# Count of candidates and casts of list and degree moved from VectorE to ScalarE, degree not clamped, replacement into a second buffer

## Chip, cores, metric

One core of a Trainium2 chip. The metric is the device time of one execution in microseconds; a profile's span is about 2 us shorter than the time of the same execution. Runs carry a state: "fast" or "slow" (over 1.5% above the fastest run of the same kernel). A ratio is the mean time of one kernel's fast runs over the mean of the other's fast runs of the same rounds, so it is not quite the ratio of the medians quoted beside it.

## The reference

One pre-norm graph-attention layer over N = 3327 nodes of width 1024. `adj` is 0/1 with few ones in a row.

```python
def reference(x, adj, Wf, bf, Wg, bg, W, bW):
    h = jnp.maximum(_layernorm(x, axis=-1), 0.0)
    f = h @ Wf + bf
    g = h @ Wg + bg
    e = jax.nn.relu(f @ g.T)
    scores = jnp.where(adj > 0, e, -9e15)
    return x + jax.nn.softmax(scores, axis=1) @ (h @ W + bW)
```

The kernel makes a list of the neighbours of each row (at most 40), sorts the rows by degree, and in part two gathers only those neighbours' rows.

## The kernel before

The change touches part one alone: 26 row tiles t0 to t25 (128 rows each, the last one 127). For each tile, `degrees` loads 128 rows of `adj`; ScalarE converts them to f32 and sums them to the degree (the "degree pass", L435); POOL multiplies by the column numbers in place (the "product", L436). `normed` is the layer norm, with small hand-overs between ScalarE and VectorE. In `edges`, VectorE searches 16 segments of the product for their 8 largest (the "searches", L446), counts the positive candidates, draws the list of 40 out of the 128 candidates by five maxima and four replacements (the "list"), and makes the list and the degree integer for a store.

```python
kpool = pool1("key", 4)     # the tiles r
cpool = pool1("cand", 2)    # cand, pos, ... : two buffers each

def normed(t):
    ...                     # even t: sums on ScalarE, odd t: statistics on VectorE
        nc.vector.bn_aggr(mv[:n], st[:n])
        nc.scalar.activation(nmr[:n], mv[:n, 0:1], AF.Copy, scale=-1.0)              # L409
    ...
    nc.vector.reciprocal(rstd[:n], rstd[:n])                                         # L419
    nc.scalar.activation(nmr[:n], nmr[:n], AF.Copy, scale=rstd[:n])                  # L420
    nc.scalar.activation(xt[:n], xt[:n], AF.Relu, bias=nmr[:n], scale=rstd[:n])      # L421
    ...

def degrees(t):
    r = kpool.tile([P, N], FP, name="r")
    ...                                                                              # load adj into r
    nc.scalar.activation(r[:n, b:e], a[:n, b:e], AF.Relu, accum_out=to)              # L435
    nc.gpsimd.tensor_mul(r[:n, b:e], r[:n, b:e], iotaj[:n, b:e])                     # L436
    ...

def edges(t, r):
    cand = cpool.tile([P, SEG * 8], FP, name="cand")
    for s in range(SEG):                                                             # SEG = 16
        nc.vector.max(cand[:n, s * 8 : s * 8 + 8], r[:n, s * SW : min(N, (s + 1) * SW)])
    pos = cpool.tile([P, SEG * 8], BF, name="pos")
    ...                                                                              # count, list, casts: see the diff

for t in range(NT):
    r = degrees(t)
    normed(t)
    edges(t, r)
    ...                                                                              # ranks, weights
```

This text is the order of tracing. The compiler's tile scheduler sorts the instructions of each engine into the queue that the engine then works off in order, so the order on the chip is not the order of these lines.

Of the kernel before, what the change touches and what calls it, by code (L numbers as in the profile page):

```python
# [8 lines left out]
FP = mybir.dt.float32  # L9
I32 = mybir.dt.int32  # L10
AF = mybir.ActivationFunctionType
ALU = mybir.AluOpType
AX = mybir.AxisListType
# [7 lines left out]
SEG = 16  # L21
KM = 40
NBIN = 64
# [266 lines left out]
def edge_path(ctx: ExitStack, tc: tile.TileContext, x, adj, Wf, bf, Wg, bg, W, bW, out, flag):  # L290
# [10 lines left out]
    nc = tc.nc  # L301
    N, D = x.shape
    O = W.shape[1]
    P = 128
# [4 lines left out]
    NT = (N + P - 1) // P  # L309
# [4 lines left out]
    def rows(t):  # L314
        return min(P, N - t * P)
# [7 lines left out]
    const = ctx.enter_context(tc.tile_pool(name="const", bufs=1))  # L323
# [10 lines left out]
    nc.gpsimd.iota(iotak, pattern=[[1, KM]], base=0, channel_multiplier=0, allow_small_or_imprecise_dtypes=True)  # L334
    ones3 = const.tile([3, P], BF, name="ones3")
    nc.gpsimd.memset(ones3, 1.0)
    bads = const.tile([P, NT + 2], FP, name="bads")
    nc.gpsimd.memset(bads, 0.0)


# [1 line left out]
    perm = const.tile([P, NT], I32, name="perm")  # L342
# [8 lines left out]
    with ExitStack() as part1:  # L351
        pool1 = lambda name, bufs, **kw: part1.enter_context(tc.tile_pool(name=name, bufs=bufs, **kw))
        c1 = pool1("c1", 1)
# [5 lines left out]
        cpool = pool1("cand", 2)  # L359
# [12 lines left out]
        iotad, lst = held[:, :NBIN], held[:, NBIN:]  # L372
# [9 lines left out]
        pay = c1.tile([P, NT, PW], I32, name="pay")  # L382
        deg = c1.tile([P, NT], FP, name="deg")
        half = c1.tile([P, 1], FP, name="half")
        cnt = c1.tile([P, NT], FP, name="cnt")
        rp = c1.tile([P, NT], FP, name="rp")
        oh = c1.tile([P, NT, NBIN], BF, name="oh")
# [53 lines left out]
        def edges(t, r):  # L441

            n = rows(t)
            cand = cpool.tile([P, SEG * 8], FP, name="cand")
            for s in range(SEG):
                nc.vector.max(cand[:n, s * 8 : s * 8 + 8], r[:n, s * SW : min(N, (s + 1) * SW)])  # L446
            pos = cpool.tile([P, SEG * 8], BF, name="pos")
            nc.vector.tensor_scalar(
                pos[:n], cand[:n], 0.0, None, op0=ALU.is_gt, op1=ALU.add, accum_out=cnt[:n, t : t + 1]
            )  # L450
            for i in range(0, KM, 8):
                nc.vector.max(lst[:n, i : i + 8], cand[:n])
                if i + 8 < KM:
                    nc.vector.match_replace(cand[:n], lst[:n, i : i + 8], cand[:n], 0.0)
            nc.vector.tensor_scalar(lst[:n], lst[:n], float(N), 1.0, op0=ALU.min, op1=ALU.max)
            nc.vector.tensor_scalar(pay[:n, t, :KM], lst[:n], -1.0, None, op0=ALU.add)
            dg = cpool.tile([P, 1], FP, name="dg")
            nc.vector.tensor_scalar(dg[:n], deg[:n, t : t + 1], float(NBIN - 1), None, op0=ALU.min)
            nc.vector.tensor_copy(pay[:n, t, KM : KM + 1], dg[:n])
            nc.vector.tensor_scalar(oh[:n, t, :], iotad[:n], dg[:n], None, op0=ALU.is_equal)  # L460

        def counted(t):

# [91 lines left out]
# [4 lines that stand above are left out]
            if t >= LAG:  # L559
                counted(t - LAG)  # L560
            if t % 4 == 3 and t > 4:
                store_lists(t - 7, t - 3)
            if t < KD:
                load_Wg(t)
            elif t < 2 * KD:
                make_A(t - KD)
            if t == 2 * KD:
                make_rows()
# [32 lines left out]
        ps = p_u.tile([P, P], FP, name="ps_u")  # L601
# [4 lines left out]
            )  # L606
        tens = c1.tile([P, NT], FP, name="tens")
        nc.vector.tensor_copy(tens, ps[:, NT : 2 * NT])
        nc.vector.scalar_tensor_tensor(perm, ps[:, :NT], float(P), tens, op0=ALU.mult, op1=ALU.add)
        over = c1.tile([P, 1], FP, name="over")  # L610
        nc.vector.tensor_scalar(over, part, float(rows(NT - 1)), float(N), op0=ALU.is_ge, op1=ALU.mult)
        nc.vector.tensor_tensor(final, perm[:, NT - 1 : NT], over, op=ALU.add)
        ne = c1.tile([P, NT], FP, name="ne")
        nc.vector.tensor_tensor(ne, deg, cnt, op=ALU.not_equal)
        nc.vector.tensor_reduce(bads[:, NT : NT + 1], ne, AX.X, ALU.max)
        nc.vector.tensor_scalar(ne, deg, 1.0, None, op0=ALU.is_lt)
        nc.vector.tensor_reduce(bads[:, NT + 1 : NT + 2], ne, AX.X, ALU.max)


    W_sb = ctx.enter_context(tc.tile_pool(name="W", bufs=1)).tile([P, KD, O], FP, name="W_sb")  # L620
# [204 lines left out]
def kernel(tc: tile.TileContext, x, adj, Wf, bf, Wg, bg, W, bW, out):  # L825



    nc = tc.nc
    with tc.tile_pool(name="flag", bufs=1) as fpool:  # L830
        flag = fpool.tile([1, 1], I32, name="flag")
        bad = edge_path(tc, x, adj, Wf, bf, Wg, bg, W, bW, out, flag)
        with tc.If(bad > 0):
            dense_path(tc, x, adj, Wf, bf, Wg, bg, W, bW, out)
# [27 lines left out]
```

## Time and profile before

| | before |
|---|---|
| time, median of 4 fast runs | 1421.8 us (1416.2 to 1423.8) |
| span of the profile, clock of TensorE granted | 1418.9 us, 0.923 |
| part one: start of the first gather on POOL | 285.9 us |
| POOL idle before its 28 products (L436) | 67.1 us |

### The profile page before, as it was taken

The page shows a single profiled execution, that of the slowest core. Times are in us where ns is not written, and L with a number is a line of the kernel's source. Part 1 is how long each engine was busy: PE and PEld are TensorE (multiplying, and loading weights), DVE is VectorE, ACT ScalarE, POOL GpSimd, SP SyncE. Part 2 cuts the span into 40 slices and gives each one's busy share as a digit, 9 for nine tenths or more (in the row PEclk, how much of TensorE's full clock was granted, in tenths as well). Part 3 has the DMA queues.
Part 4 walks back from the last instruction along what each step waited for, and adds up shares of the span by engine and source line. Part 5 has one row for each costly group of instructions (what it writes and reads, how often), then busy time and mean ns, then how long its engine had stood idle before and what let it go on. Part 6 is the DMA issues. An engine that isn't in the chain of part 4 may idle for free.

```text
span 1418.9 us, 14086 instructions
## 1 busy us (share of the span) xinstructions
PE 1176.7 (83%) x4355; PEld 686.1 (48%) x4355; DVE 1252.2 (88%) x2602; ACT 444.5 (31%) x686; POOL 872.4 (61%) x628
## 2 busy tenths in 40 slices
PE   4569998177298989999978987999999998999676
PEld 3544454044165556665545554555555554555332
DVE  4888889929979999998889889999999998999991
ACT  6666776311053134433302322212222111111100
POOL 8677777265666776665556546567666765656500
PEclk9999999578599999999989998999999998999788
DMA  9897796197677988886687567788887876788700
GB/s 370 334 361 301 290 350 220 48 368 269 223 286 265 328 313 310 285 277 245 233 308 280 201 236 274 271 297 297 279 288 245 266 251 224 245 281 264 256 31 32
DMA packets 97709, 372.51 MB, mean 263 GB/s; under 512 B 14268, under 2 KB 14684, under 8 KB 94297
## 3 DMA queue, kind: packets, MB, share of 16 engines
q0 software_dynamic: 79552, 286.85, 58.0%
q1 hardware_dynamic: 10860, 70.49, 13.1%
q10 hardware_dynamic: 7212, 14.18, 2.8%
q8 instruction: 36, 0.59, 0.2%
q14 instruction: 49, 0.40, 0.1%
HBM read 343.67 MB, written 27.80 MB: 262 GB/s over the span
## 4 chain that ended last, share of the span: by engine, by line
PE 28%; DVE 25%; issue 22%; POOL 15%; DMA 6%; ACT 2%; POOLq 0%; ACTq 0%; SPq 0%; DVEq 0%
PE ps_o L760 14%; DVE y L746 13%; POOL r L436 10%; PE ps_q L666 8%; DVE junk L683 6%; PE yT_ps L724 4%; POOL G L638 4%; DMA G<-hd,pi 4%; DVE cand L446 2%; PE ps_A L519 1%; DVE xp L768 1%; DVE sc L683 1%; DMA pi<-pd,perm 1%; ACT r L435 1%; PE ps_o L761 1%
## 5 line engine op out<-in xcount | busy, mean ns | idle before, releaser
L638 POOL DMA_INDIRECT G<-hd,pi x468 | 555.6, 1187 | 319.3 <-ACT y L744 105.9
L683 DVE CUSTOM_DVE_ANT_0 junk<-G,q 128x1024 bf16<-128x1024 f32 x468 | 600.6, 1283 | 41.4 <-DMA G<-hd,pi 21.6
L666 PE MATMUL ps_q<-A_sb,hT 128*128 128x342 f32 x1248 | 395.9, 467 | 58.1 <-ACT q L668 44.5
L746 DVE SCALAR_TENSOR_TENSOR y<-G,sc,y 128x1024 f32<-128x1024 f32 x320 | 411.2, 1285 | 4.4 <-ACT y L744 2.8
L760 PE MATMUL ps_o<-W_sb,yT 128*128 128x512 f32 x832 | 388.2, 621 | 10.2 <-ACT yT L755 9.9
L666 PEld LDWEIGHTS ps_q<-A_sb,hT 128*128 128x128 f32 x1248 | 233.5, 194 | 178.6 <-ACT q L668 46.3
L760 PEld LDWEIGHTS ps_o<-W_sb,yT 128*128 128x128 f32 x832 | 161.2, 198 | 209.4 <-issue 190.7
L436 POOL TENSOR_TENSOR r<-r,iotaj 128x3327 f32<-128x3327 f32 (+4 forms) x28 | 188.6, 6742 | 67.1 <-ACT r L435 53.1
L446 DVE MAX8 cand<-r 128x8 f32<-128x208 f32 (+2 forms) x416 | 134.2, 359 | 35.6 <-POOL r L436 35.6
L668 ACT COPY q<-ps_q 128x342 f32<-128x342 f32 x78 | 32.8, 449 | 326.2 <-DVE sc L683 234.6
L740 ACT ACTIVATE G<-G,sc 128x1024 f32<-128x1024 f32 x122 | 129.0, 1136 | 0.0
L519 PE MATMUL ps_A<-WgT,WfT 128*128 128x512 f32 x256 | 120.7, 633 | 1.1 <-ACT WfT L490 1.0
L724 PE MATMUL yT_ps<-ident,G 128*128 128x128 f32 x976 | 117.5, 277 | 2.4 <-ACT G L740 2.4
L724 PEld LDWEIGHTS yT_ps<-ident,G 128*128 128x128 f32 x976 | 107.5, 141 | 15.1 <-ACT G L740 7.3
L650 ACT COPY hT<-ps_t 128x512 f32<-128x512 f32 x52 | 30.2, 593 | 193.8 <-PE ps_q L666 162.9
L755 ACT COPY yT<-yT_ps 128x512 f32<-128x512 f32 x52 | 27.8, 586 | 194.3 <-PE yT_ps L724 194.3
L519 PEld LDWEIGHTS ps_A<-WgT,WfT 128*128 128x128 f32 x256 | 51.3, 203 | 65.0 <-issue 62.7
L724 PE MATMUL yT_ps<-ident,y 128*128 128x128 f32 x208 | 34.6, 321 | 52.8 <-DVE y L746 31.9
L435 ACT ACTIVATE r<-r 128x3327 f32<-128x3327 int32 (+4 forms) x28 | 77.5, 2766 | 0.1
L769 POOL DMA_INDIRECT out_dram<-xp,perm x25 | 31.8, 1271 | 59.4 <-DVE xp L768 50.9
L768 DVE TENSOR_TENSOR xp<-ps_o,xp 128x512 f32<-128x512 f32 x52 | 35.6, 685 | 36.0 <-PE ps_o L761 35.7
L724 PEld LDWEIGHTS yT_ps<-ident,y 128*128 128x128 f32 x208 | 28.7, 166 | 57.4 <-DVE y L746 34.6
(139 smaller groups left out, 781.0 us busy)
## 6 DMA issues: line engine op xcount, KB each, us to landing
r<-in_adj_dram SPq DMA_DIRECT2D x25, 1663.5 KB, 9.5
xt<-in_x_dram SPq DMA_DIRECT2D x25, 512.0 KB, 9.7
hd<-xt ACTq DMA_DIRECT2D x25, 512.0 KB, 6.1
G<-hd,pi POOLq DMA_INDIRECT x468, 6.1
wr<-in_L_gnn_Wg_dram SPq DMA_DIRECT2D x8, 512.0 KB, 13.8
wr<-in_L_gnn_Wf_dram SPq DMA_DIRECT2D x8, 512.0 KB, 8.9
W_sb<-in_L_gnn_W_dram SPq DMA_DIRECT2D x1, 4096.0 KB, 16.9
r<-in_adj_dram SPq DMA_DIRECT2D x1, 1455.6 KB, 8.7
```

Source lines behind the costliest of these rows:

```text
L435: nc.scalar.activation(r[:n, b:e], a[:n, b:e], AF.Relu, accum_out=to)
L436: nc.gpsimd.tensor_mul(r[:n, b:e], r[:n, b:e], iotaj[:n, b:e])
L446: nc.vector.max(cand[:n, s * 8 : s * 8 + 8], r[:n, s * SW : min(N, (s + 1) * SW)])
L519: nc.tensor.matmul(ps, WfT[:, k, :], WgT[:, k, o * CB : (o + 1) * CB], start=(k == 0), stop=(k == KD - 1))
L638: nc.gpsimd.indirect_dma_start(out=to, out_offset=None, in_=table, in_offset=bass.IndirectOffsetOnAxis(ap=idx, axis=0),)
L666: nc.tensor.matmul(ps[:, :QB], hT[:, k, :], A_sb[:, k, o : o + QB], start=(k == 0), stop=False)
L683: nc.vector.tensor_tensor_reduce(junk, g, e["q"][:, :D], 1.0, e["q"][:, D : D + 1], op0=ALU.mult, op1=ALU.add, accum_out=e["sc"][:, k : k ...
L724: nc.tensor.matmul(e["yT"][:, c, :], g[:, c * P : (c + 1) * P], ident, is_transpose=True, start=(first and c % 4 == 0), stop=(last and c % ...
L740: nc.scalar.activation(g, g, AF.Copy, scale=p)
L746: nc.vector.scalar_tensor_tensor(y, g, p, y, op0=ALU.mult, op1=ALU.add)
L760: nc.tensor.matmul(ps, yT[:, k, :], W_sb[:, k, o * CB : (o + 1) * CB], start=(k == 0), stop=False)
L768: nc.vector.tensor_add(xo, e["o"][o], xo)
```

## The change

Intent: relieve VectorE, which had 232.6 us of work in the 286 us of part one, by giving the count and two casts to ScalarE, and free `cand` from being overwritten, so that ScalarE can count while VectorE draws the list. The clamp of the degree goes; one clamp and one check at the end of part one take its place.

```diff
             pos = cpool.tile([P, SEG * 8], BF, name="pos")
-            nc.vector.tensor_scalar(
-                pos[:n], cand[:n], 0.0, None, op0=ALU.is_gt, op1=ALU.add, accum_out=cnt[:n, t : t + 1]
-            )
+            rest = cpool.tile([P, SEG * 8], FP, name="rest")
+            nc.scalar.activation(pos[:n], cand[:n], AF.Sign, accum_out=cnt[:n, t : t + 1])
+            of = cand
             for i in range(0, KM, 8):
-                nc.vector.max(lst[:n, i : i + 8], cand[:n])
+                nc.vector.max(lst[:n, i : i + 8], of[:n])
                 if i + 8 < KM:
-                    nc.vector.match_replace(cand[:n], lst[:n, i : i + 8], cand[:n], 0.0)
-            nc.vector.tensor_scalar(lst[:n], lst[:n], float(N), 1.0, op0=ALU.min, op1=ALU.max)
-            nc.vector.tensor_scalar(pay[:n, t, :KM], lst[:n], -1.0, None, op0=ALU.add)
-            dg = cpool.tile([P, 1], FP, name="dg")
-            nc.vector.tensor_scalar(dg[:n], deg[:n, t : t + 1], float(NBIN - 1), None, op0=ALU.min)
-            nc.vector.tensor_copy(pay[:n, t, KM : KM + 1], dg[:n])
-            nc.vector.tensor_scalar(oh[:n, t, :], iotad[:n], dg[:n], None, op0=ALU.is_equal)
+                    nc.vector.match_replace(rest[:n], lst[:n, i : i + 8], of[:n], 0.0)
+                    of = rest
+            ids = cpool.tile([P, KM], FP, name="ids")
+            nc.vector.tensor_scalar(ids[:n], lst[:n], float(N), 1.0, op0=ALU.min, op1=ALU.max)
+            nc.scalar.activation(pay[:n, t, :KM], ids[:n], AF.Copy, bias=-1.0)
+            nc.scalar.copy(pay[:n, t, KM : KM + 1], deg[:n, t : t + 1])
+            nc.vector.tensor_scalar(oh[:n, t, :], iotad[:n], deg[:n, t : t + 1], None, op0=ALU.is_equal)
 ...
+        nc.vector.tensor_scalar(perm, place_of, float(N - 1), None, op0=ALU.min)
 ...
+        nc.vector.tensor_scalar(ne, deg, float(NBIN), None, op0=ALU.is_ge)
+        nc.vector.tensor_reduce(bads[:, NT + 2 : NT + 3], ne, AX.X, ALU.max)
```

More of the change, by code (lines that the diff above doesn't have):

```diff
@@ L336, in edge_path @@
     nc.gpsimd.memset(ones3, 1.0)
-    bads = const.tile([P, NT + 2], FP, name="bads")
+    bads = const.tile([P, NT + 3], FP, name="bads")
     nc.gpsimd.memset(bads, 0.0)
@@ L608, in edge_path @@
         nc.vector.tensor_copy(tens, ps[:, NT : 2 * NT])
-        nc.vector.scalar_tensor_tensor(perm, ps[:, :NT], float(P), tens, op0=ALU.mult, op1=ALU.add)
+        place_of = c1.tile([P, NT], FP, name="place_of")
+        nc.vector.scalar_tensor_tensor(place_of, ps[:, :NT], float(P), tens, op0=ALU.mult, op1=ALU.add)
+        nc.vector.tensor_scalar(perm, place_of, float(N - 1), None, op0=ALU.min)
         over = c1.tile([P, 1], FP, name="over")
```

## The prediction

> **What bounds the kernel now.** I read the page's slices and groups first, then the waits of the first 260 us, then the timelines of POOL and ScalarE there. The change touches only the first part (26 row tiles, t0 to t25: degrees, candidate lists, placing). That part ends when the first gather of part two starts on POOL, at 285.9 us of the 1418.9 us span. No engine is full in it:
>
> ```profile
> span 1418.9 us, 14086 instructions
> ...
> L436 POOL TENSOR_TENSOR r<-r,iotaj 128x3327 f32<-128x3327 f32 (+4 forms) x28 | 188.6, 6742 | 67.1 <-ACT r L435 53.1
> L446 DVE MAX8 cand<-r 128x8 f32<-128x208 f32 (+2 forms) x416 | 134.2, 359 | 35.6 <-POOL r L436 35.6
> ...
> L435 ACT ACTIVATE r<-r 128x3327 f32<-128x3327 int32 (+4 forms) x28 | 77.5, 2766 | 0.1
> ```
>
> After the bar stand busy time, mean ns, then idle time before the group and its main cause. POOL multiplies each tile by the column numbers in 7.2 us and stands idle 67 us in all, 53 of them until ScalarE's degree pass (L435) has made the tile. DVE takes maxima of POOL's product. So each tile runs ACT, POOL, DVE. The waits say why ScalarE, which is less busy still, is late:
>
> ```profile
> POOL r L436 <- ACT r L435: 53.1, 18, 6.0
> DVE cand L446 <- POOL r L436: 35.2, 14, 3.7
> ...
> ACT nmr L420 <- DVE rstd L419: 20.9, 8, 5.9
> ...
> ACT nmr L409 <- DVE mv L408: 14.9, 5, 4.0
> ```
>
> (total us, times, longest.) ScalarE itself waits for small DVE results, the reciprocal `rstd` and the mean `mv` of the layer norm, which stand in DVE's queue behind maxima that need POOL. That is a loop through three in-order queues. Its two kinds of step show in the timelines (start, length):
>
> ```profile
> 29.81 7.26 POOL L436 TENSOR_TENSOR r<-r,iotaj 128x3327 f32<-128x3327 f32 x1 [1.90 <-ACT r L435]
> 37.49 7.23 POOL L436 TENSOR_TENSOR r<-r,iotaj 128x3327 f32<-128x3327 f32 x1 [0.42 <-ACT r L435]
> 49.92 7.26 POOL L436 TENSOR_TENSOR r<-r,iotaj 128x3327 f32<-128x3327 f32 x1 [5.19 <-ACT r L435]
> 57.60 7.22 POOL L436 TENSOR_TENSOR r<-r,iotaj 128x3327 f32<-128x3327 f32 x1 [0.42 <-DVE cand L446]
> 70.05 7.25 POOL L436 TENSOR_TENSOR r<-r,iotaj 128x3327 f32<-128x3327 f32 x1 [5.23 <-ACT r L435]
> ```
>
> ```profile
> 34.36 2.96 ACT L435 ACTIVATE r<-r 128x3327 f32<-128x3327 int32 x1
> 37.23 0.19 ACT L435 ACTIVATION_READ_ACCUMULATOR r<-r 128x1 f32 x1
> 40.60 0.29 ACT L420 ACTIVATE nmr<-nmr,rstd 128x1 f32<-128x1 f32 x1 [3.19 <-DVE rstd L419]
> ...
> 46.50 0.20 ACT L409 ACTIVATE nmr<-mv 128x1 f32<-128x1 f32 x1 [3.51 <-DVE mv L408]
> 46.60 0.28 ACT L410 ACTIVATE rstd<-mv,eps 128x1 f32<-128x1 f32 x1
> 46.79 2.96 ACT L435 ACTIVATE r<-r 128x3327 f32<-128x3327 int32 x1
> ```
>
> POOL runs in pairs: t2 and t3 back to back, a gap of 5.2 us, t4 and t5 back to back, a gap. The first of a pair pays the loop (POOL 7.3, DVE's maxima of t2 up to the statistics of t3, 9.3 us from 37.1 to 46.4, ScalarE 3.4: 20.1 us per pair). The second does not, because the degree pass of t3 (34.36) is queued **ahead** of the `nmr` of t2 (40.60) that waits for DVE. That place in the queue is what I look for in the changed kernel.
>
> **What the Trainium skill says.** "Perfetto Trace Analysis", Tensor Engine Instruction, says of the other engines that "ACT/DVE/GPSIMD are strict FIFO"; the trace agrees, for at 40.60 ScalarE stood 3.2 us with later work ready. The same page, GPSIMD Engine Instruction, says to time POOL by the spacing of starts: two back-to-back passes took 14.45 us, so 7.2 each, like the recorded 7.24. "ScalarE: Activation LUTs", What ACT_TABLE_LOAD costs, gives an immediate-operand ACTIVATE 186 ns + 0.833 ns per element (estimates for the new ones below); the trace's 128x1 `nmr` took 0.19 to 0.20. It gives 1283 ns for a load, as both loads here took; the changed build has no more loads than before, so Sign shares the set in use.
>
> **The change part by part.** Taken off DVE per tile, by spacing of starts: count (L448) 0.20 us, integer list 0.10, degree clamp and cast about 0.15 together. About 0.45 us, x26 = 12 us. The clamp of the list stays, and the second buffer takes the same match and replace. Put on ScalarE per tile: Sign over 128 columns 0.29 (estimate) plus its accumulator read 0.19 (as for L435), the list's cast 0.22 (estimate), the degree copy 0.15 (as L526): about 0.8 us, some 0.7 with overlap, x26 = 18 us on an engine busy 13.7 of 20 us. At the end come one more 128x26 operation on `perm` and one more check: three or four small DVE operations between the last list and the gathers, about 0.8 us. Part two has the same order on every engine in both builds: 0.
>
> The larger effect is order. The compiled queues of the changed kernel differ all through part one, because the tile scheduler has re-sorted them:
> - ScalarE's degree pass of t3 now comes **after** `nmr` of t2, whose `rstd` DVE makes seven maxima and four replacements into t2, so after POOL's t2.
> - The pass of t4 comes after the cast of t2's list, which DVE finishes three maxima into t3, so after POOL's t3. Those of t7, t11, t15, t17, t20 and t23 likewise come behind the cast of the list two tiles back; those of t8, t12 and t16 come behind the Sign count of the tile just before, and that of t19 behind the count of t17, which need all 16 maxima of that tile.
> - On DVE more lists are worked out with no maxima between: a max/replace pair then takes 0.73 us from start to start (152.22 to 152.95) and not 0.46.
>
> So POOL, DVE, ScalarE, POOL run in series more often. I followed the queues by hand with the trace's spacings: POOL 7.25; maxima 0.28; a max of the list 0.19 and a replacement 0.27 between maxima, the pair 0.73 alone; one half of statistics 0.6; degree pass 2.96 to 3.15; `xt` 1.14; PSUM copy 0.5. For t3: POOL ends t2 at 36.9; seven maxima, four replacements, three list maxima 3.6, so 40.5; `nmr` 0.2; degree pass 3.1; POOL starts t3 at 43.8, where it was 37.5. For t8: POOL ends t7 at 95.3; 16 maxima 4.5 and the list's end 0.3, so 100.1; Sign 0.3; pass 3.1; t8 starts at 103.5, after an idle of 8.2 us, where it was 89.1. POOL starts in this way (before, then changed): t4 49.9, 57.4; t6 70.1, 74.3; t7 77.7, 88.0; t10 108.4, 120.7; t12 128.5, 148.7; t14 148.9, 163.2 (t13 and t14 follow without gap); t16 166.9, 194.7; t19 194.5, 222.8; t21 212.8, 244.0; t23 232.9, 270.1; end of t25 264.7, 299.8. From there to the gather 21.2 us, now about 21 (a little less DVE work, the 0.8 us more). Part one so ends near 321 and not 286: **+35 us**, with the savings in it. I take 34.
>
> **The rivals.** *DVE's saving tells:* if the new order did no harm, 12 us of DVE work off a loop that contains it gives at best 1410. For it: the 9.3 us of DVE are in the loop of a pair, and the intent. Against: the degree passes behind new waits. *ScalarE's load alone:* 0.7 us per tile fully on the path gives 1440; fully hidden gives about 1421. Against it as the whole story: ScalarE idles about 6 of 20 us now. *The queues bite less:* each wait could end earlier than I reckon, if DVE is ahead; a shift of 15 to 20 us gives 1437 to 1442. *PE as a new bound:* the product WgT.WfT keeps PE nearly full from 100 to 240; its weights' copies are late too, and waits for `pre` on DVE could add 5 to 10 us more.
>
> **Range and chances.** 1421.9 + 34 = 1456. Two per cent is 28 us, so slower ends above 1450.3. My errors: about 0.3 us in each of some 15 gaps, partly of one sign, and a gap or two misread (6 us each): about 9 us either way. Range 1440 to 1470. Slower by over 2% 0.70, within 2% 0.28, faster 0.02.
>
> **What would show it.** In the changed profile POOL's idle before L436 should rise from 67 to about 100 us, with gaps of 5 to 9 us before t3, t4, t7, t8, t11, t12, t15, t16, t19, t20 and t23, still put down to ScalarE's pass; ScalarE's `nmr`, list casts and counts should carry waits on DVE of several us just ahead of those passes; DVE should wait for POOL longer than 35 us though its work fell by some 10; the part from the first gather on should last as before, within 5 us. I am wrong if the first gather starts before about 300 us, if POOL's t3 follows t2 within 2 us, or if ScalarE shows table loads at Sign (then slower by far more).

## The result, and the profile after

Slower. The changed kernel took 1461.97 us (median of 4, 1458.2 to 1462.4), against 1421.8; ratio of the fast runs 1.0283, 95% interval 1.0249 to 1.0317. The span was 1460.1 us at a clock of 0.919.

Where the time came from, first: POOL's first gather and its wait, in the timeline of before and then of after.

```profile
285.89 1.07 POOL L638 DMA_INDIRECT hp<-hd,perm  x1 [21.20 <-DVE final L612]
```

```profile
321.36 1.07 POOL L644 DMA_INDIRECT hp<-hd,perm  x1 [20.99 <-DVE final L616]
```

Part one became 35.5 us longer. The rest went from 1133.0 to 1138.7 us. The tail between the last product and the gather kept its 21 us. Next, the page of after: the span, then groups with busy time, mean ns, idle time and releaser.

```profile
span 1460.1 us, 14060 instructions
...
L436 POOL TENSOR_TENSOR r<-r,iotaj 128x3327 f32<-128x3327 f32 (+4 forms) x28 | 188.0, 6730 | 103.4 <-ACT r L435 88.8
L446 DVE MAX8 cand<-r 128x8 f32<-128x208 f32 (+2 forms) x416 | 126.7, 362 | 63.0 <-POOL r L436 63.0
...
L435 ACT ACTIVATE r<-r 128x3327 f32<-128x3327 int32 (+4 forms) x28 | 77.5, 2768 | 0.4 <-ACT pay L459 0.4
```

The products cost the same, but POOL stood idle 103.4 us before them, 36.3 more than before: that is the whole lengthening of part one. The waits of the first 300 us of after (us in total, times, longest) say for what:

```profile
POOL r L436 <- ACT r L435: 88.8, 14, 9.5
DVE cand L446 <- POOL r L436: 63.0, 25, 6.2
...
ACT pay L459 <- DVE ids L458: 46.4, 15, 7.3
...
ACT pos L450 <- DVE cand L446: 22.6, 13, 4.6
ACT nmr L420 <- DVE rstd L419: 22.4, 10, 5.4
```

ScalarE now waits 46.4 us for finished lists (`pay`, the cast) and 22.6 us for finished candidates (`pos`, the count). Neither wait existed before. POOL's starts for t2, t3, t4, t7 and t8 (start, length, idle before), and ScalarE at t3, t4 and t8:

```profile
29.51 7.21 POOL L436 TENSOR_TENSOR r<-r,iotaj 128x3327 f32<-128x3327 f32 x1 [1.71 <-ACT r L435]
43.86 7.20 POOL L436 TENSOR_TENSOR r<-r,iotaj 128x3327 f32<-128x3327 f32 x1 [7.14 <-ACT r L435]
57.37 7.23 POOL L436 TENSOR_TENSOR r<-r,iotaj 128x3327 f32<-128x3327 f32 x1 [6.31 <-ACT r L435]
...
87.76 7.20 POOL L436 TENSOR_TENSOR r<-r,iotaj 128x3327 f32<-128x3327 f32 x1 [6.50 <-ACT r L435]
103.28 14.42 POOL L436 TENSOR_TENSOR r<-r,iotaj 128x3327 f32<-128x3327 f32 x2 [8.32 <-ACT r L435]
```

```profile
40.53 0.29 ACT L420 ACTIVATE nmr<-nmr,rstd 128x1 f32<-128x1 f32 x1 [3.28 <-DVE rstd L419]
40.73 2.96 ACT L435 ACTIVATE r<-r 128x3327 f32<-128x3327 int32 x1
...
51.84 0.29 ACT L420 ACTIVATE nmr<-nmr,rstd 128x1 f32<-128x1 f32 x1 [5.44 <-DVE rstd L419]
...
54.23 2.98 ACT L435 ACTIVATE r<-r 128x3327 f32<-128x3327 int32 x1 [0.36 <-ACT pay L459]
...
99.84 0.31 ACT L450 ACTIVATE pos<-cand 128x128 bf16<-128x128 f32 x1 [1.47 <-DVE cand L446]
100.06 0.19 ACT L450 ACTIVATION_READ_ACCUMULATOR pos<-cand 128x1 f32 x1
100.15 2.96 ACT L435 ACTIVATE r<-r 128x3327 f32<-128x3327 int32 x1
```

At 40.73 the degree pass of t3 starts the moment the `nmr` of t2 has got its reciprocal; before, the same pass ran at 34.36, ahead of that `nmr`. The pass of t4 (54.23) stood behind the `nmr` of t3, which waited 5.44 us; the cast of t2's list just before the pass (53.65) then ran without a wait. At 100.15 the pass of t8 follows at once on the count of t7. The waits of after list no degree pass that waited for its load of `adj`: only the place in the queue holds the pass.

VectorE has 127 fewer instructions in part one, and its busy time there went from 232.6 to 234.2 us, not down. The timelines show why: of the 104 list steps (a maximum and its replacement), 5 stood alone before and 41 do after, with no other VectorE instruction between its parts, and a step alone takes 0.73 us from start to start, against 0.46 of its own when it alternates with searches. 36 steps by 0.27 us are 9.7 us, which eats most of the 12 that were saved.

### The profile page after: what moved, and what is told of

Same layout as the page of the kernel before. It is cut to its first block, busy times and chain, and to the rows that moved or that the text cites. A ratio compares the mean times of both kernels' runs of the same rounds, so it can differ in the third digit from the quotient of the medians.

```text
span 1460.1 us, 14060 instructions
## 1 busy us (share of the span) xinstructions
PE 1178.4 (81%) x4355; PEld 685.9 (47%) x4355; DVE 1253.8 (86%) x2475; ACT 459.9 (32%) x790; POOL 872.5 (60%) x628
## 4 chain that ended last, share of the span: by engine, by line
PE 28%; DVE 24%; issue 21%; POOL 16%; DMA 7%; ACT 4%; POOLq 0%; ACTq 0%; SPq 0%; DVEq 0%
PE ps_o L766 16%; DVE y L752 11%; POOL r L436 9%; PE ps_q L672 7%; POOL G L644 5%; DVE junk L689 5%; DMA G<-hd,pi 4%; PE yT_ps L730 4%; DVE cand L446 3%; DMA pi<-pd,perm 1%; ACT r L435 1%; ACT G L746 1%; DVE xp L774 1%; DVE sc L689 1%; DVE rest L455 1%
## 5 line engine op out<-in xcount | busy, mean ns | idle before, releaser
L436 POOL TENSOR_TENSOR r<-r,iotaj 128x3327 f32<-128x3327 f32 (+4 forms) x28 | 188.0, 6730 | 103.4 <-ACT r L435 88.8
L446 DVE MAX8 cand<-r 128x8 f32<-128x208 f32 (+2 forms) x416 | 126.7, 362 | 63.0 <-POOL r L436 63.0
```

## Experiments

**Theory.** The loss is not the cost of the new instructions but the places that the scheduler gave the degree passes: behind ScalarE instructions that wait for VectorE, which waits for POOL. **Rivals:** the new ScalarE instructions cost it by themselves; one part of the change carries it all; VectorE's order carries it.

They ran on three other occasions, on chips where the kernel before had medians of 1487, 1497 and 1486 us and often fell into the slow state, so totals there are weak evidence. Each verdict rests on part one, read from one trace for each run. Three of these traces are of slow executions (new operations two ahead, in the best order, and held). In the kernels that ran again, all traced in fast executions, part one kept within 0.8 us while the traced execution's total moved by up to 15.6 us, so I read part one from all traces alike; but no kernel was traced in both states.

### Old operations in the new order, new operations in the old order

Both kernels compute as before and after do. A table holds the queues of TensorE, SyncE, VectorE and ScalarE in part one to the other kernel's order, by dependencies that bind the order of issue and add no wait. An instruction that the other kernel lacks was put where its inputs were there already (on ScalarE mostly behind the next degree pass). In kernels with such a table the lines of part one have higher numbers: L476 and L470 are the degree pass, L477 and L471 the product.

```diff
+        for engine, runs in QUEUES.items():        # per engine: part one's instructions, in the wished order
+            ...
+            for first, then in zip(at, at[1:]):
+                tc.add_manual_dep(mine[then], mine[first].name, issue_order, reason="queue order")
```

> The changed kernel's operations, with the instructions of every engine in part one held to the order of the kernel before (the Sign counts and casts are put on ScalarE at places where their input is already there, behind the next degree pass). My theory (the re-sorted queues cost the 35 us, the operations themselves are worth a little): part one 278 us, so 8 below the kernel before, total about 1413, ratio to before 0.994 (0.988 to 1.002). Rival (ScalarE's added 0.7 us per tile is what costs, wherever it is queued): part one 300 or more, total 1436 or more, ratio 1.01 or more. POOL's idle ahead of the product: theory 55 to 70 us, rival 80 or more.

> The kernel before, none of its operations changed, with the instructions of every engine in part one held to the order that the changed kernel has for the same instructions (no Sign count and no cast stands on ScalarE, so the waits at those are not there). If only the places of the common instructions matter: as slow as the changed kernel, ratio 1.025 to 1.03. If only the waits of the new ScalarE instructions matter: ratio 1.00. My estimate is between: the gaps before t3, t4, t12, t20 stay, those before t7, t8, t16 and t17 go or shrink, so part one 300 to 315, total about 1442, ratio 1.014 (1.007 to 1.024).

POOL's starts of t2, t3 and t4, first with the new operations in the old order, then with the old operations in the new order:

```profile
29.41 7.26 POOL L477 TENSOR_TENSOR r<-r,iotaj 128x3327 f32<-128x3327 f32 x1 [1.70 <-ACT r L476]
37.48 7.23 POOL L477 TENSOR_TENSOR r<-r,iotaj 128x3327 f32<-128x3327 f32 x1 [0.81 <-ACT r L476]
48.82 7.25 POOL L477 TENSOR_TENSOR r<-r,iotaj 128x3327 f32<-128x3327 f32 x1 [4.11 <-ACT r L476]
```

```profile
29.55 7.23 POOL L471 TENSOR_TENSOR r<-r,iotaj 128x3327 f32<-128x3327 f32 x1 [1.92 <-ACT r L470]
43.92 7.20 POOL L471 TENSOR_TENSOR r<-r,iotaj 128x3327 f32<-128x3327 f32 x1 [7.14 <-ACT r L470]
57.40 14.43 POOL L471 TENSOR_TENSOR r<-r,iotaj 128x3327 f32<-128x3327 f32 x2 [6.28 <-ACT r L470]
```

The gap follows the order, not the operations. With the new operations in the old order part one was 287.5 us; I had expected 278, as the lighter VectorE should have helped, so that half is a miss: on balance they neither cost nor gain. The balance holds a new wait: VectorE stood idle 8.1 us, in four waits, until ScalarE's count had read a `cand` buffer (more on this below). Whether the 8 us gained in my expectation went there is not shown. With the old operations in the new order it was 305.6, in the expected range, with the same 7.14 us before t3 as the changed kernel. So the order of the instructions that both kernels share makes 19.7 of the 35.5 us. The other 15.8, by subtraction, are the new instructions' waits in that order. The table held both queues, so no run separates the share of ScalarE's order from that of VectorE's. Totals: 1496.6 us (1492.2 to 1507.2, 5 fast runs) and 1502.6 (1499.1 to 1513.9, 5 fast runs), with a single fast run of the kernel before beside them. Run again for the total, five rounds on another chip:

> The kernel of new_ops_old_order once more, for the total. Theory: part one 286 to 289 us, total within 10 us of the kernel before among fast runs.

Part one 287.2 us, total 1489.2 (1469.8 to 1494.2), ratio to before 0.994 (0.988 to 1.001): the same. The new operations in the old order are not slower; the 2.8% are gone.

### One half of the change at a time

The count on ScalarE with the second buffer, alone in the kernel before, in whatever order the scheduler then chose:

```diff
-            nc.vector.tensor_scalar(pos[:n], cand[:n], 0.0, None, ..., accum_out=cnt[:n, t : t + 1])
+            nc.scalar.activation(pos[:n], cand[:n], AF.Sign, accum_out=cnt[:n, t : t + 1])
-                    nc.vector.match_replace(cand[:n], lst[:n, i : i + 8], cand[:n], 0.0)
+                    nc.vector.match_replace(rest[:n], lst[:n, i : i + 8], of[:n], 0.0)
```

And the two casts with the unclamped degree alone:

```diff
-            nc.vector.tensor_scalar(pay[:n, t, :KM], lst[:n], -1.0, None, op0=ALU.add)
-            nc.vector.tensor_scalar(dg[:n], deg[:n, t : t + 1], float(NBIN - 1), None, op0=ALU.min)
-            nc.vector.tensor_copy(pay[:n, t, KM : KM + 1], dg[:n])
+            nc.scalar.activation(pay[:n, t, :KM], ids[:n], AF.Copy, bias=-1.0)
+            nc.scalar.copy(pay[:n, t, KM : KM + 1], deg[:n, t : t + 1])
```

> The kernel before with the count on ScalarE and the second buffer alone; clamps and casts as before. In the compiled queue the degree pass of tile 3 stands again ahead of the scaling of tile 2, but that of tile 8 behind the whole row path of tile 7. Theory (the loss is the re-sorting, and it needs particular positions): part one 288 to 305 us, the gap at tile 3 gone, one left at tile 8. Rival (the count itself, waiting for its candidates in ScalarE's queue, is the cost): part one 310 us or more, gaps before the products behind a count.

> The kernel before with list cast, degree cast and unclamped degree alone; count on VectorE in one buffer as before. Theory (re-sorting): part one 288 to 305 us; the two halves need not add to 35. Rival (the casts alone carry the loss): part one 315 us or more; rival (they cost nothing): 284 to 288 us.

The count alone: part one 288.2 us, POOL's gap before t3 3.2 us (7.1 in the changed kernel, 0.4 before, so not quite gone), the one before t8 6.4 us; total 1494.1, ratio 1.012 (0.999 to 1.025), unclear. The casts alone: part one 304.3 us, total 1510.6, ratio 1.026 (1.005 to 1.046), unclear too. Both lengths as the theory had them. The halves add 2.3 and 18.4 us, 20.7 together; the whole adds 35.5. A part therefore has no cost of its own that could be added up: each combination was sorted anew.

### Degree passes two tiles ahead

If the place of the pass is the loss, tracing it earlier should help both kernels.

```diff
+        ready = {}
         for t in range(NT):
-            r = degrees(t)
+            for u in range(t, min(NT, t + 3)):
+                if u not in ready:
+                    ready[u] = degrees(u)
             normed(t)
-            edges(t, r)
+            edges(t, ready.pop(t))
```

> The changed kernel with the degree passes written two tiles ahead of the lists, so that the scheduler queues the pass of a tile on ScalarE ahead of the waits for the two tiles before it. Theory (the loop POOL, DVE, ScalarE, POOL is broken): POOL's gaps fall to under 2 us each, and DVE, at about 8.2 us per tile, or the transfers set the pace; part one about 252 us, total 1390, ratio 0.977 (0.965 to 0.99). Rival (DVE and ScalarE are simply too full with the new operations): no better than the kernel before, ratio 1.00 or more.

> The kernel before with the same two-tile lead of the degree passes and none of the changed operations. Theory: DVE sets the pace and has 0.45 us more per tile than in the changed kernel with the lead, so part one about 10 us longer than there: total 1400, ratio 0.985 (0.975 to 0.995). Rival (PE's products or the transfers set the pace once the loop is gone): the same as the changed kernel with the lead within 4 us, and the changed operations are worth nothing.

Old operations: part one 257.7 us, as expected. POOL's idle time fell from 67.1 to 29.7 us. The stretch from 40 to 80 us, from the windows (its length, then busy time and instructions of TensorE, its weight loads, VectorE, ScalarE, POOL; clock, DMA share, GB/s):

```profile
40.00:80.00 40.00, 25.93 (x120) 24.18 (x118) 40.00 (x203) 34.77 (x51) 37.31 (x6) 1.00 1.01 397
```

VectorE is busy for all 40 us and the DMA engines too: here other limits come up. Its total was 1456.7 (1443.1 to 1468.5, 4 runs, two fast). Repeated twice:

> The same kernel as old_ops_ahead, for its total on another occasion. Theory: part one again 255 to 260 us against 286, and the total 20 to 32 us below the kernel before in runs of the same state. Rival (part two gives it back: its gathers start earlier but wait for the same thing): total within 10 us of the kernel before.

> The kernel of old_ops_ahead once more, for a verdict on the total with more rounds. Theory: part one 255 to 260 us, total 22 to 32 us (1.5 to 2.2%) below the kernel before among fast runs.

Part one was 257.0 and 257.1 us. Totals: 1466.2 (1450.3 to 1477.1) with ratio 0.997 (0.981 to 1.014), undecided among few fast runs; then, with six fast runs against eight, 1456.0 (1447.5 to 1466.3) beside 1486.5 (the median of all eleven), ratio 0.981 (0.976 to 0.985). So it is faster than the kernel before, by about 1.9%; whether by 2% is unclear, as the interval lies on both sides of 0.98. That is near the 28.8 us by which part one is shorter: there is no sign that part two gives it back. It is the best version.

New operations: part one 281.4 us where I expected 252. A miss: ScalarE's `nmr` waited 36.0 us for reciprocals in it (9.3 with the old operations), and degree passes stood behind those waits. Total 1489.7 (1458.8 to 1492.1), one fast run of four. So I held the small instructions back.

### Holding small ScalarE instructions behind degree passes

The scalings of the row mean, the count and the casts of tile t go behind the degree pass of t+3 (with the lead of two tiles), or of t+1 (without a lead), again by issue order alone. The degree pass is L440 there, the product L441.

```diff
-            nc.scalar.activation(nmr[:n], nmr[:n], AF.Copy, scale=rstd[:n])
+            behind(t, nc.scalar.activation(nmr[:n], nmr[:n], AF.Copy, scale=rstd[:n]))   # likewise L409, Sign, casts
 ...
+        for t, ins in waiting:
+            if t + 3 < NT:                                                               # or t + 1
+                tc.add_manual_dep(ins.ins, passes[t + 3].ins.name, issue_order, reason="queue order")
```

> The new operations, with degree passes traced two tiles ahead and every small ScalarE instruction that waits for VectorE (the two row-mean scalings, the count, the two casts) put in ScalarE's queue behind the degree pass three tiles later, by issue order alone, no wait added. Theory (a degree pass standing in ScalarE's queue behind an instruction that waits for VectorE is the whole loss, and once none does, the lighter VectorE lists show): POOL's idle time before its products falls from 103 us to under 35, part one (start of the first gather) ends at 240 to 258 us. Rival 1 (the new operations cost something of their own, a longer list on VectorE or readers of the second buffer): POOL's gaps go but part one stays above 265 us. Rival 2 (the gaps come from elsewhere, such as the adjacency loads): POOL still idles over 60 us before products and part one ends above 280 us.

> The change as it is, no lead, but the row-mean scalings, the count and the two casts of tile t stand in ScalarE's queue behind the degree pass of tile t+1; VectorE's order is left to the compiler, which now runs the lists of many tiles with few searches between their steps. Theory A (ScalarE's queue alone holds the loss): the gap at tile 3 gone and part one at 275 to 290 us. Theory B (ScalarE's queue holds part of it, and VectorE's list steps, 0.73 us a pair when they stand alone and 0.46 us between searches, the rest): part one at 292 to 312 us with VectorE's searches as the releaser of POOL or of ScalarE. Rival (neither): 316 us or more.

With t+3 POOL's idle time fell to 41.6 us and part one to 269.7: better than 281.4, but over the 240 to 258 expected, so rival 1 was the nearer one. In its trace 56 of the 104 list steps stand alone, and reciprocals stand behind whole lists, so that a chain of ScalarE waits remains (`nmr` for `rstd`: 25.2 us, 11 times). Total 1483.8 us (1453.6 to 1497.1), again one fast run of four. Holding ScalarE's queue made the scheduler sort VectorE's anew.

With t+1 and no lead, part one was 307.0 us and the ratio 1.011 (1.006 to 1.017; 1503.5 us, 1501.3 to 1508.5): within 2% of before, on the slow side. The number lies in theory B's range; its trace gives another reason than the one named there. POOL's products of t4 and t5, VectorE between them, then ScalarE:

```profile
49.45 7.24 POOL L441 TENSOR_TENSOR r<-r,iotaj 128x3327 f32<-128x3327 f32 x1 [2.47 <-ACT r L440]
62.64 7.22 POOL L441 TENSOR_TENSOR r<-r,iotaj 128x3327 f32<-128x3327 f32 x1 [5.96 <-ACT r L440]
```

```profile
56.72 0.38 DVE L451 MAX8 cand<-r 128x8 f32<-128x208 f32 x1 [2.04 <-POOL r L441]
```

```profile
58.71 0.24 ACT L464 ACTIVATE pay<-ids 128x40 int32<-128x40 f32 x1 [2.95 <-DVE ids L463]
...
59.50 2.98 ACT L440 ACTIVATE r<-r 128x3327 f32<-128x3327 int32 x1
```

Here is one turn of the loop. VectorE had begun the list of t3, then came to a search of t4, which had to wait for POOL to end t4 (56.69). Then it finished the list (58.5), ScalarE cast it (58.71), and only then came the pass of t5, and POOL. The cast that I had moved behind one pass had landed ahead of the next.

### New operations in the best order

To take both queues out of the scheduler's hands, the new operations were held to the queues of the best kernel (old operations, lead of two), as in the first experiment; the count was put behind a degree pass.

> The new operations, two tiles ahead, with every queue of part one held to the order in which the old operations were compiled with the same lead (the order of old_ops_ahead), the moved count and casts put where their inputs are there already. Theory (the orders of ScalarE's and VectorE's queues decide, the operations themselves do not): part one 250 to 260 us, POOL's idle time before products under 35 us, where the compiler's own order of the same operations gave 281 and 270 us. Rival (the new operations cost something of their own, more waits of ScalarE or longer lists): part one above 266 us.

Part one 279.9 us: a miss by 20, and the rival's number. The total was 1481.3 (1465.6 to 1490.0), ratio 0.993 (0.988 to 0.999): within 2% of the kernel before. The trace shows, larger, the cost of 8.1 us met in the first experiment. A search on VectorE, then ScalarE's queue, then a line of the waits:

```profile
64.43 0.38 DVE L489 MAX8 cand<-r 128x8 f32<-128x208 f32 x1 [6.68 <-ACT pos L493]
```

```profile
60.97 2.98 ACT L478 ACTIVATE r<-r 128x3327 f32<-128x3327 int32 x1 [1.56 <-DMA r<-in_adj_dram]
...
63.95 0.29 ACT L493 ACTIVATE pos<-cand 128x128 bf16<-128x128 f32 x1
```

```profile
DVE cand L489 <- ACT pos L493: 13.6, 4, 6.7
```

`cand` has two buffers. Once ScalarE does the count, VectorE may not write the next tile's candidates into a buffer until ScalarE has read it. At 57.75 (64.43 less the wait) VectorE was ready; the count stood behind a pass that waited for its load; VectorE lost 6.7 us, and 13.6 us in four such waits (4.9 more on the cast of a degree). So "the operations cost nothing, the order all" is not shown for every order. The candidates of that count were complete at 50.86, when VectorE began the list of the same tile, so an earlier place on ScalarE was open to it. Whether an earlier place, or a third candidate buffer, removes the waits was not run and stays open, and so is how much of the 22 us to the old operations with the same lead they explain.

### All together

| kernel | POOL idle before products | wait before the gather | part one |
|---|---|---|---|
| before | 67.1 | 21.2 | 285.9 |
| after | 103.4 | 21.0 | 321.4 |
| old operations, new order | 86.5 | 22.0 | 305.6 |
| new operations, old order (first run) | 68.7 | 21.4 | 287.5 |
| count alone | 70.5 | 20.3 | 288.2 |
| casts alone | 86.7 | 20.2 | 304.3 |
| held behind the next pass | 89.4 | 20.3 | 307.0 |
| new, two ahead | 62.4 | 21.5 | 281.4 |
| new, in the best order | 46.4 | 36.1 | 279.9 |
| new, two ahead, held | 41.6 | 30.6 | 269.7 |
| old, two ahead (first run) | 29.7 | 30.3 | 257.7 |

Part one moves with POOL's idle time, us for us, until POOL runs so far ahead that VectorE has lists left over when the last product is done: then the wait before the gather grows by 9 to 15 us.

## Why the prediction was right

- **The order as the main effect: right.** Part one +35.5 us, predicted +35. POOL's starts by hand against the trace: t3 43.8 and 43.86, t4 57.4 and 57.37, t8 103.5 and 103.28, t16 194.7 and 194.82, t23 270.1 and 269.08. The step "degree pass behind `nmr`" is borne out by the run of the old operations in the new order. That run has no count and no cast on ScalarE; for these the evidence is the waits just ahead of the passes (2.79 us at the cast before t7, 1.47 at the count before t8) and the run of the new operations in the old order.
- **The instruction that holds each pass: right for ten of eleven.** For t4 the prediction named the cast of t2's list; the trace has the wait at the `nmr` of t3 (5.44 us), and the old operations in the new order, without any cast on ScalarE, start t4 at 57.40 too. Both results come from VectorE behind its first search of t3 (51.10 us; reciprocal 51.65, list 52.46), so the loop is the predicted one, but that the start of t4 came out right to 0.03 us is partly luck.
- **The places of the gaps: right.** All eleven tiles named have gaps of 5.0 to 9.5 us; one at t24 (9.4 us) was not named. The profile puts ten of the eleven down to ScalarE's pass, as predicted, and that of t16 down to VectorE. Idle time 103.4 us against "about 100".
- **The new ScalarE work: slightly over.** Its busy time in part one rose by 15.3 us (181.0 to 196.3), predicted 18. Sign took 0.31 us (0.29), list cast 0.23 (0.22), degree cast 0.18 (0.15). As a cause by itself it is ruled out by the new operations in the old order.
- **VectorE's 12 us of savings: mis-sized.** They did not appear: busy time in part one +1.6 us. The prediction saw the list steps that stand alone but did not set them against the saving; they are 9.7 us. "Its work fell by some 10" is wrong, while "waits for POOL longer than 35 us" (63.0) is right.
- **Part two unchanged "within 5 us": just missed.** It took 5.7 us more, with the same order on every engine. The kernel before varies by 7.7 us from run to run, and the new operations in the old order, whose part one is 1.3 us over before's, had a total like before's. I take it for such variation, but that is not shown. With it the total is 6.0 us over the predicted 1456 and inside the range.
- **Rivals.** VectorE's saving telling (1410) and ScalarE's load alone (1440) fell with the new operations in the old order. TensorE as the new bound: no sign of it. VectorE waited 0.9 us in all for TensorE's `pre` in part one, 1.4 before.

## What to carry to other kernels

Moving an instruction to a less busy engine puts a wait for the giving engine into the taking engine's in-order queue; ask what stands behind it there, and whether the giving engine needs that to go on. Where a scheduler sorts the queues, compare the compiled orders before timing: here the order alone moved part one by 20 us with the old operations and by 34 us with the new, and tracing a feeding pass two tiles early won 28 us. A reader on a second engine also holds the buffer: count the buffers before moving it.

## What the Trainium skill lacked or had wrong

- "VectorE: DVE Perf Modes" names the maximum of eight and the match-and-replace pair but gives no time for them by name. Here: 0.36 us recorded for a 128x208 maximum, 0.28 from start to start; a list step over 128 columns 0.73 alone and 0.46 of its own between searches. Steps that stand alone cost 0.27 us more each, 41 of 104 in the changed kernel.
- "ScalarE: Activation LUTs", What ACT_TABLE_LOAD costs, was right: its formula gives 0.29 us for Sign over 128 columns and 0.22 for the cast over 40; measured 0.31 and 0.23, and no added load.
- "Perfetto Trace Analysis", Tensor Engine Instruction, says that these engines' queues are strictly first in, first out, and the traces agree; no page says that a change of operations can re-sort the compiled queues, nor how to compare them. Here that alone was 19.7 us of part one.
- No page that I found treats a buffer whose reader moves to another engine; the nearest is a general remark on buffer counts behind repeated gaps in "Perfetto Trace Analysis", Optimization Strategy. Here, with two candidate buffers, VectorE waited up to 6.7 us.
